# A four-layer graph kernel: layer 0's rows from unscaled relu rows and composite weights, two row blocks begun together, and a listed order

## The chip, the cores and the metric

The kernel runs on one core of one Trainium2 chip. The core has a matrix engine (TensorE, PE in the profile, with its weight loads as PEld), a vector engine (VectorE, DVE), a scalar engine (ScalarE, ACT), a general engine (GpSimd, POOL) and a queue for transfers (SyncE, SP). Each engine works through its own list of instructions in the order in which the program issued them; semaphores make one engine wait for another. The metric is the device time of one execution in microseconds (us). The kernel before takes 595.72 us (median of three runs, 595.17 to 596.13).

## The reference

There are 4096 nodes with 64 features and a sparse 4096 x 4096 matrix of ones and zeros, `adj`. Four layers follow each other, each of the form `x = x + f(relu(layernorm(x)), adj)`. The change touches layer 0 alone:

```
h  = maximum(layernorm(x), 0)
h  = lorentz_linear(h, W,  b,  scale)       # 4096 x 64
q  = lorentz_linear(h, Wq, bq, scale_q)
k  = lorentz_linear(h, Wk, bk, scale_k)
att = adj * sigmoid((2 + 2 * qm @ k.T) / att_scale + att_bias)   # qm: q, column 0 negated
support = att @ h
x = x + support / sqrt(abs(support[:, 0]**2 - sum(support[:, 1:]**2)))
```

`lorentz_linear` multiplies by a 64 x 64 matrix, adds a bias, makes of column 0 a "time" `t = sigmoid(h0) * exp(scale) + 1.1`, and scales columns 1 to 63 so that the sum of their squares is `t*t - 1`. So a positive factor on all of the 63 columns ahead of that scaling is of no consequence to them; the time needs the unscaled column 0. Layer 1 multiplies a counted and decayed `adj` with `h @ weight`, layer 2 multiplies `adj` with `h`, layer 3 averages over neighbours.

## The kernel before

The 4096 rows lie as 32 tiles of 128 rows (`x_sb`, 128 x 32 x 64). A block `ib` is 512 rows (four tiles), and there are eight; a chunk `g` is two tiles of columns, and there are sixteen. The transposed matrix is read from DRAM as tiles of 128 x 1024 for one (block, chunk); GpSimd's queue loads them as one-byte masks (`load_masks`, L180), which stay on the chip for all four layers. Another copy is read by SP's queue to check that all entries are 0 or 1 (`check`, L361); a general program for other matrices stands behind an `If` and is not entered.

**Rows ahead of layer 0** (`before0`, twice: for row tiles 16 to 31, then 0 to 15). Mean, variance and scaling of the rows on VectorE; a transpose to PSUM and a copy (`ht`); a product with W, to which a bf16 split of the biases (`bias_rows`, on GpSimd) is added by a product with ones; factors (`factors`, `root`); `fb` (L758), the rows of h; a second transpose (`hq`) and the product with Wq and Wk together; factors again; query rows into `q_sb` and key rows `kr` (L805); a third transpose into `kt`. The queries of a block are turned by `queries_turned` (L874) and laid out by `queries_laid` (L884).

**Attention of layer 0.** For each (block, chunk): `scores` (L938, PE), `sigmoids` (L951, ACT), `masked` (L962, DVE, a product with the mask), `gather` (L969, PE, into one accumulator per block). I call one `scores` or one `gather` of a (block, chunk) a unit; layer 0 has 128 of each, 256 units. The first block (7) and two units of scores of block 6 stand in a listing with the rows: each part has a planned duration, its predecessors and the PSUM places that it takes, and `Listing.run` tries 2500 random priorities against those planned durations and emits the best plan. Planned idle time of PE is filled with products nobody reads (`idle`, L1062), at first fifty of them. All other units come from a loop, four at a time, with four gathers behind four scores.

**Jobs.** What follows a block is a generator pushed on `jobs` with a lag; `step()` runs the first job to its next `yield` and goes on to the second only when the first has had as many steps as its lag. After a block of attention it is `rows0(ib)` (lag 10): transposes of the accumulator (L236), halves added, the norm of the support, an inverse root on GpSimd (`rsqrt`, L261 to L268: twelve small instructions), the layer norm for layer 1 with a second such root, and `split` (L250, L253), which writes the block's rows for layer 1 into `s2a`. The loop makes one step per unit of scores. Behind layer 0, `chunks_counted` makes eight steps, and layer 1 one step per pass. `need(1, t)` makes steps at once until the block of row tile t is there.

**Layer 1.** Blocks go in pairs; a pass handles two row tiles, from 31 down to 0, of both blocks: products `cnt` (L1260, L1270), the weights `w` (L1284 on DVE, L1286 on ACT), and, one pass late, products `acc` (L1298) with `s2a`. So block 0, finished last in layer 0, is needed last, in the fifteenth products of the first pair.

Of the kernel before, what the change touches and what calls it, by code (L numbers as in the profile page):

```python
# [11 lines left out]
F32 = mybir.dt.float32  # L12
# [27 lines left out]
UP, STEP = 2.0**23, 2.0**11  # L40

# [9 lines left out]
def kernel(  # L51
# [57 lines left out]
    nc.scalar.activation(tried, exp_s[:, 0:1], AF.Sqrt)  # L109
# [29 lines left out]
    def model(general):  # L139
# [9 lines left out]
        HR = 8  # L149
# [5 lines left out]
        def rows_in(gr):  # L155
# [10 lines left out]
        todo = [  # L166
            (ib, g) for ib in order0 for g in (first_cols if ib == order0[0] else range(NG))
        ]
# [201 lines left out]
        pp = pool("pp0", 2, l0, space=PSUM)  # L370
# [3 lines left out]
        for gr in range(1, len(ROWS)):  # L374
            rows_in(gr)
        if not general:
            more_in()

        brow = pro.tile([P, 3 * D], BF16, name="brow" + sfx)
        ones = pro.tile([P, P], BF16, name="ones" + sfx)
        nc.vector.memset(ones, 1.0)

        def bias_rows():
            v = vec[:, V_B : V_B + 3 * D]
            sel = pro.tile([P, 3], F32, name="sel" + sfx)
            high = pro.tile([P, 3 * D], BF16, name="high" + sfx)
            left, part = (
                pro.tile([P, 3 * D], F32, name=f"brow_{a}{sfx}") for a in ("left", "part")  # L390
            )
            total = pro.tile([P, 3 * D], F32, name="brow_sum" + sfx)
            nc.gpsimd.tensor_tensor(sel, ident[:, 0:3], ident[:, D : D + 3], ALU.add)
            for n in range(3):
                nc.gpsimd.tensor_copy(high, v if n == 0 else left)
                to = total if n == 0 else part
                nc.gpsimd.tensor_scalar(to, high, sel[:, n : n + 1], None, ALU.mult)
                if n:
                    nc.gpsimd.tensor_tensor(total, total, part, ALU.add)
                if n < 2:  # L400
                    nc.gpsimd.tensor_tensor(left, v if n == 0 else left, high, ALU.subtract)
            nc.gpsimd.tensor_copy(brow, total)

        class Listing:
# [5 lines left out]

            HOP, TURN, TRIALS = 0.15, 0.12, 2500

# [13 lines left out]
            def plan(self, names, lead):  # L426

                busy, forms, places = {}, {}, dict.fromkeys(names, 0.0)
                at = [part.at for part in self.parts]
                open_ = [len(part.after) for part in self.parts]  # L430
                able = [part for part in self.parts if not part.after]
                where, order, last = {}, [], 0.0
                while able:
                    best = None
                    for part in able:
                        free_at = busy.get(part.engine, 0.0)
                        if forms.get(part.engine) != part.form:
                            free_at += self.TURN
                        t, place = max(at[part.n], free_at), None
                        if part.takes:  # L440
                            free = [(places[n], n) for n in part.takes if places[n] is not None]
                            if not free:
                                continue
                            since, place = min(free)
                            t = max(t, since + self.HOP)
                        if best is None or t - lead[part.n] < best[0]:
                            best = t - lead[part.n], t, part, place
                    _, t, part, place = best
                    if place is not None:
                        places[place] = None  # L450
                    where[part.n] = place
                    part.idle = t - busy.get(part.engine, 0.0)
                    end = busy[part.engine] = t + part.us
                    forms[part.engine] = part.form
                    last = max(last, end)
                    if part.frees is not None:
                        places[where[part.frees.n]] = end
                    able.remove(part)
                    order.append(part)
                    for q in part.then:  # L460
                        at[q.n] = max(at[q.n], end + self.HOP)
                        open_[q.n] -= 1
                        if not open_[q.n]:
                            able.append(q)
                assert len(order) == len(self.parts)
                return last, order, where

            def run(self, names, fill):

                draw = random.Random(1)  # L470
                lead = [0.0] * len(self.parts)
                best = self.plan(names, lead)
                for _ in range(self.TRIALS):
                    other = list(lead)
                    for _ in range(draw.randint(1, 4)):
                        other[draw.randrange(len(other))] = draw.uniform(-2.0, 2.0)
                    plan = self.plan(names, other)
                    if plan[0] <= best[0]:
                        best, lead = plan, other
                self.plan(names, lead)  # L480
                for part in best[1]:
                    part.place = best[2][part.n]
# [3 lines left out]
        def root(y, a, tag):  # L486
# [7 lines left out]
            for share, to in ((SHARE, z), (0.25, y)):  # L494
                nc.vector.reciprocal(q, z)
                nc.vector.scalar_tensor_tensor(q, q, share, a, ALU.mult, ALU.mult)
                nc.vector.tensor_tensor(to, q, z, ALU.add)

        tables, flats = [], []

        TURN = ("pm", "pa")

        def turn_tile(part, name, shape=(P, CI, P)):
            on, tag = (pm, "pr") if part.place == "pm" else (pa0, "pa")
            return on.tile(list(shape), F32, tag=tag, name=name + sfx)

        def before0(todo, gr, bias):
# [13 lines left out]
            def of(u, n=1):  # L521
                return slice(u * HR * n, (u + 1) * HR * n)

# [3 lines left out]
            def numbers(name, n=1):  # L527
                return small(f"{name}{gr}", "", pro, R * n)


            def begin(_):
                v.st, v.va = numbers("st"), numbers("va")
                v.xc, v.sq = buffer("A", "xc", [P, R, D]), buffer("B", "sq", [P, R, D])

            def mean(u):
                def emit(_):
                    if u == 0:
                        begin(_)
# [3 lines left out]
            def scaled(_):  # L542
                nc.vector.tensor_scalar(v.st, v.st, -1.0 / D, None, ALU.mult)

            def centred(u):
                return lambda _: nc.vector.tensor_tensor(
                    v.xc[:, of(u), :], x_sb[:, rows(u), :], bc(v.st[:, of(u)], HR), ALU.add
                )

            def squared(to, frm, part):  # L550
                return lambda _: nc.scalar.activation(
                    getattr(v, to)[:, part, :], getattr(v, frm)[:, part, :], AF.Square
# [6 lines left out]

            def rooted(_):  # L560
                v.rs = numbers("rs")
# [1056 lines left out]
```

## Time and profile before

| | |
|---|---|
| timed runs, median of 3 | 595.72 us (595.17 to 596.13) |
| the profiled execution, first to last instruction | 593.2 us |
| what lies around the span (median less span) | 2.5 us |
| PE busy | 577.5 us (97%) |
| DVE, ACT, POOL busy | 477.9, 337.7, 242.7 us |
| first fifty `idle` products | 1.58 to 15.00 us |
| first scores | 47.83 us |
| block 7 done, loop begins | 83.31 us |
| first `many` (layer 1's counts) | 297.46 us |
| first layer-1 pass | 312.09 us |
| last products of the first pair | 347.37 us |

A row of the timeline is: start, duration, engine, line, operation, tile written and tiles read, size, count. A duration with a count above one is that of the whole stretch. In brackets stands the idle time before and who ended it. PE is nearly always busy, but its busy time includes the `idle` products, and a matmul's end is modelled; what the stage is worth is read from when the useful units run.

### The profile page before, as it was taken

To read this page: it belongs to the slowest core of one execution; us is meant where nothing else is said; L and a number is where in the kernel's file an instruction comes from. 1 tells how busy PE (TensorE), PEld (TensorE's weight loads), DVE (VectorE), ACT (ScalarE), POOL (GpSimd) and SP (SyncE) were. 2 spreads that over 40 slices of the span, in tenths; PEclk is the share of its full clock that TensorE was granted. 3 is DMA by queue.
4 is the path that set the end of the run, shared out by engine and by line. 5 is a ranking of instruction groups with operands and counts; after the bars stand their busy time and mean duration, and the time that the engine had idled before them with its cause. 6 is when DMAs were issued, how large, how long until landed. Compare 5 with 4: busy or idle time off the path is not lost.

```text
span 593.2 us, 9215 instructions
## 1 busy us (share of the span) xinstructions
PE 577.5 (97%) x3138; PEld 238.6 (40%) x3138; DVE 477.9 (81%) x909; ACT 337.7 (57%) x546; POOL 242.7 (41%) x459
## 2 busy tenths in 40 slices
PE   8999999999999999999999999999998999999995
PEld 3663333333333333333243343343443545544553
DVE  5679666899989899999876878879888669987753
ACT  3678666667676776767427677767666014431221
POOL 7625204657767676744434201001010305562352
PEclk9999999999999999999999999999999999999999
DMA  9995932898999899962191545555555486546921
GB/s 148 131 106 45 102 30 18 82 151 136 168 150 166 144 158 153 149 145 88 42 349 38 173 153 189 167 173 177 166 191 181 151 271 200 161 172 210 312 83 42
DMA packets 43016, 87.04 MB, mean 147 GB/s; under 512 B 5136, under 2 KB 22032, under 8 KB 42960
## 3 DMA queue, kind: packets, MB, share of 16 engines
q1 hardware_dynamic: 23808, 68.40, 35.3%
q0 software_dynamic: 18720, 17.57, 31.8%
q8 instruction: 26, 0.43, 0.3%
q10 hardware_dynamic: 432, 0.40, 0.3%
q14 instruction: 30, 0.25, 0.1%
HBM read 135.63 MB, written 1.05 MB: 230 GB/s over the span
## 4 chain that ended last, share of the span: by engine, by line
PE 77%; DVE 10%; POOL 6%; issue 3%; ACT 3%; DMA 1%; DVEq 0%; POOLq 0%; ACTq 0%
PE acc L1370 19%; PE ps L938 12%; PE acc L969 11%; PE acc L1298 10%; PE cnt L1260 9%; DVE att L962 4%; PE cnt L1270 3%; PE idle L1062 3%; PE many L1193 2%; PE pt L236 2%; POOL mask L180 1%; PE pr L1173 1%; POOL rs_a L265 1%; DVE ck L361 1%; PE pn L1447 1%
## 5 line engine op out<-in xcount | busy, mean ns | idle before, releaser
L361 DVE SCALAR_TENSOR_TENSOR ckw<-ckw 128x1024 f32<-128x1024 f32 x98 | 124.5, 1278 | 5.5 <-DMA ckw<-adjt_dram 5.3
L938 PE MATMUL ps<-qt,kt 64*128 64x512 f32 x512 | 123.2, 610 | 2.9 <-DVE att L962 2.5
L969 PE MATMUL acc<-att,fb 128*64 128x512 f32 x512 | 117.8, 599 | 0.6 <-DVE att L962 0.5
L1286 ACT ACTIVATE w<-cnt 128x512 int16<-128x512 f32 x176 | 93.1, 597 | 42.3 <-PE cnt L1270 41.9
L962 DVE TENSOR_TENSOR att<-ps,mask 128x1024 f32<-128x1024 f32 x82 | 98.4, 1217 | 8.4 <-ACT ps L951 8.3
L951 ACT ACTIVATE ps<-ps,att_c,att_a 128x1024 f32<-128x1024 f32 x82 | 93.5, 1177 | 1.5 <-PE ps L938 1.3
L951 ACT ACTIVATE att<-ps,att_c,att_a 128x1024 f32<-128x1024 f32 x46 | 54.6, 1203 | 59.0 <-PE ps L938 58.8
L180 POOL DMA_DIRECT2D mask<-adjt_dram x128 | 70.1, 558 | 19.7 <-DMA mask<-adjt_dram 18.2
L938 PEld LDWEIGHTS ps<-qt,kt 64*128 64x128 f32 x512 | 45.1, 186 | 77.9 <-issue 32.9
L1284 DVE TENSOR_SCALAR w<-cnt 128x512 int16<-128x512 f32 x80 | 53.6, 687 | 23.2 <-PE cnt L1270 21.8
L962 DVE TENSOR_TENSOR att<-att,mask 128x1024 f32<-128x1024 f32 x46 | 56.6, 1246 | 18.1 <-ACT att L951 18.1
L1260 PE MATMUL cnt<-mask,after 128*128 128x512 fp8e4 x256 | 66.3, 379 | 1.9 <-DVE w L1284 1.4
L1298 PE MATMUL acc<-w,s2a 128*128 128x512 bf16 x256 | 66.5, 382 | 0.1
L280 POOL TENSOR_TENSOR xc<-x_sb,st 128x256 f32<-128x256 f32 x24 | 20.0, 832 | 110.1 <-DVE st L277 70.8
L969 PEld LDWEIGHTS acc<-att,fb 128*64 128x64 f32 x512 | 33.5, 136 | 73.0 <-issue 67.5
L1370 PE MATMUL acc<-mask,s2a 128*128 128x512 fp8e4 x256 | 57.8, 379 | 0.0
L1370 PE MATMUL acc<-mask,s2b 128*128 128x512 fp8e4 x256 | 57.7, 379 | 0.0
L265 POOL TENSOR_TENSOR rs_a<-rs_y 128x4 f32<-128x4 f32 x48 | 18.2, 378 | 69.2 <-DVE rs_y L261 66.7
L361 DVE SCALAR_TENSOR_TENSOR ck<-ck 128x512 f32<-128x512 f32 x60 | 43.1, 718 | 0.0
L1260 PEld LDWEIGHTS <-after 128*128 128x128 bf16 x256 | 24.8, 99 | 30.8 <-issue 3.4
L1370 PEld LDWEIGHTS <-s2b 128*128 128x128 f16 x256 | 25.0, 98 | 27.6 <-issue 0.8
L1370 PEld LDWEIGHTS <-s2a 128*128 128x128 f16 x256 | 24.6, 98 | 27.3
(198 smaller groups left out, 606.3 us busy)
## 6 DMA issues: line engine op xcount, KB each, us to landing
ckw<-adjt_dram SPq DMA_DIRECT2D x98, 512.0 KB, 3.5
mask<-adjt_dram POOLq DMA_DIRECT2D x128, 128.0 KB, 9.0
ck<-adjt_dram SPq DMA_DIRECT2D x60, 256.0 KB, 5.9
x_sb<-x_dram SPq DMA_DIRECT2D x4, 256.0 KB, 7.7
out_dram<-y POOLq DMA_DIRECT2D x6, 128.0 KB, 2.2
out_dram<-y ACTq DMA_DIRECT2D x2, 128.0 KB, 2.2
w_sb<-wts_dram SPq DMA_DIRECT2D x2, 80.0 KB, 7.6
vec<-vecs_dram ACTq DMA_DIRECT2D x1, 130.5 KB, 6.3
```

Source lines behind the costliest of these rows:

```text
L180: nc.gpsimd.dma_start(out=masks[ib][:, g * CG : (g + 1) * CG, :], in_=adjt[ib, g])
L265: nc.gpsimd.tensor_tensor(a, y, y, ALU.mult)
L361: nc.vector.scalar_tensor_tensor(at, at, 0.0, at, ALU.not_equal, ALU.not_equal, accum_out=odd[:, k : k + 1])
L938: nc.tensor.matmul(ps[:, c, :], kt[half, g, :], qts[ib][half, :], start=True, stop=True)
L951: nc.scalar.activation(to, ps, AF.Sigmoid, bias=att_c, scale=att_a)
L962: nc.vector.tensor_tensor(att, frm, mask, ALU.mult)
L969: nc.tensor.matmul(acc[c * D : (c + 1) * D, :], lhs[:, t, :], rhs[:, c, :], start=(at == 0), stop=(at == NG - 1), skip_group_check=True,)
L1260: nc.tensor.matmul(cnt, after, masks[ib][:, t, :], start=True, stop=True, skip_group_check=True)
L1284: nc.vector.tensor_scalar(w, cnt, 0.0, None, ALU.max)
L1286: nc.scalar.activation(w, cnt, AF.Relu)
L1298: nc.tensor.matmul(accs[ib], both(s2a, t), w, start=(t == NT - 1), stop=False, skip_group_check=True,)
L1370: nc.tensor.matmul(acc, both(s2, t), masks[ib][:, t, :], start=(t == 0), stop=(t == NT - 1), skip_group_check=True,)
```

## The change

Four things change together.

1. **Rows.** The layer norm's scale is no longer applied. The centred rows are turned at once, relu is taken on the way out of PSUM (`positive`), and the result `r` is multiplied both with W and with composite weights `both_w` = W (column 0 left out) times [Wq, Wk], made by `weights_made` on the chip. What the missing factors would have given is added by small products: the numbers `al` (standard deviation, time, and a common factor) are turned (`numbers_turned`), and multiplied with `spread`, which GpSimd builds from the biases and rows of Wq and Wk. The second transpose (`hq`) goes; two transposes of numbers come. `bias_rows` goes.
2. **The square root** of the variance is no longer ACT's Sqrt but `root` on DVE, so ACT loads one table less in this stage.
3. **Two blocks together.** The listing now holds the sixteen (block, chunk) of blocks 7 and 6 on the first eight chunks, then block 7 on the other eight, and two more scores: 26 units of scores and 24 of gather. Block 6's accumulator holds the PSUM place `pm` meanwhile, so `rows0` of block 7 is held back (`waiting`) until block 6 is done; then both are pushed, with a lag of 16 instead of 10.
4. **The order** of the listing is not planned but read from a list of part numbers, `ORDER`.

The queue of SP gets four small broadcasts (`extra`) ahead of the four loads of `wxn_sb`.

```
+ORDER = (268, 8, 270, 1, 0, 269, 267, 266, 271, 273, 274, 9, 2, 10, 13, 3, 11, 20, 4, 5, 21, ...)
...
-    nc.scalar.activation(tried, exp_s[:, 0:1], AF.Sqrt)
+    nc.scalar.activation(tried, exp_s[:, 0:1], AF.Sigmoid)
...
-        todo = [
-            (ib, g) for ib in order0 for g in (first_cols if ib == order0[0] else range(NG))
-        ]
+        LEAD, FIRST = 2, 24
+        half_cols = [first_cols[: NG // 2], first_cols[NG // 2 :]]
+        todo = [(ib, g) for cols in half_cols for ib in order0[:LEAD] for g in cols]
+        todo += [(ib, g) for ib in order0[LEAD:] for g in range(NG)]
...
+            for j, row in ((1, wts[0:1, W_QK : W_QK + 2 * D]), (2, vecs[:, V_BQK : V_BQK + 2 * D])):
+                nc.sync.dma_start(
+                    out=extra[s + j * CR : s + (j + 1) * CR, :], in_=row.to_broadcast([CR, 2 * D])
+                )
...
+            tail = todo.add("DVE", 0.1, tail, at=1.5)
+            picked = todo.add("POOL", 0.6, picks, at=1.6)
+            for_u = todo.add("POOL", 2.4, spread_out(slice(0, D), vec[:, V_B : V_B + D]), picked, at=7.2)
+            turn = todo.add("PE", 0.5, turn_w, at=8.0, takes=TURN)
+            laid = todo.add("DVE", 0.3, lay_w, turn, tail, frees=turn)
+            product = todo.add("PE", 0.6, multiply_w, laid, takes=TURN)
+            done = todo.add("ACT", 0.9, lay_ww, product, frees=product)
+            for_v = todo.add("POOL", 4.6, spread_out(slice(D, 3 * D), extra), done, picked)
...
+                if lead:
+                    xc.append(add("DVE", 0.7, centred(u), ms[u]))
+                else:
+                    m = add("POOL", 0.2, scaled(u), ms[u])
+                    xc.append(add("POOL", 1.6, centred(u), m))
+            sq = [add("ACT", 0.62, squared(u), xc[u]) for u in HALF]
+            va = [add("DVE", 0.68, variance(u), sq[u]) for u in HALF]
+            va = add("DVE", 0.18, varied, *va)
+            sds = add("DVE", 1.55, rooted, va)
...
+                t = add("PE", 0.5, turned_half(lambda u: v.xc[:, of(u), :], u, "h"), xc[u], takes=TURN)
+                r.append(add("ACT", 0.6, positive(u), t, frees=t))
...
+            hb = add("PE", 1.0, h_added, sT, hs[1], const.for_u)
...
+            sq = [add("ACT", 0.6, h_squares(s), hb) for s in range(2)]
+            zf = add("DVE", 0.2, h_first, *sq, rs)
+            sg = add("ACT", 0.22, h_sigmoid, zf)
...
+            tm = add("DVE", 0.8, h_times, sg)
+            gg = add("DVE", 1.75, h_ratio, tm, *nm)
+            al = add("DVE", 0.2, h_numbers, gg, st)
...
+                pv.append(
+                    add("PE", 1.15, products(u), r[u], const.both, *pv[-1:], takes=WIDE)
+                )
+                vb.append(add("PE", 0.6, added(u), pv[u], aT, const.for_v))
...
             acc, late = first_rows_and_block()
-            push(rows0(order0[0], evacuated(order0[0], acc, 0)), 10)
+            waiting = [(order0[0], evacuated(order0[0], accs[order0[0]], 0))]
...
-            first = [2] * 7 if general else [4, 4, 3, 3]
+            first = [2] * 3 if general else [3, 3]
...
                     if at == NG - 1:
-                        push(rows0(ib, evacuated(ib, acc, 0)), 10)
+                        waiting.append((ib, evacuated(ib, accs[ib], 0)))
+                        for done in waiting:
+                            push(rows0(*done), 16)
+                        waiting = []
```

## The prediction

> **What bounds the kernel now.** I read the busy time by stretches first. Its columns are the stretch, its length, then PE, PEld, DVE, ACT and POOL with their counts, the granted clock, the DMA share and GB/s.
>
> ```profile
> 60.00:80.00 20.00, 19.94 (x86) 6.30 (x88) 12.80 (x11) 12.54 (x14) 4.22 (x8) 1.00 1.02 94
> ...
> 312.00:442.00 130.00, 129.54 (x741) 51.53 (x738) 106.87 (x205) 92.08 (x178) 17.78 (x40) 1.00 0.48 157
> ```
>
> PE bounds both layer 0's attention and layer 1 (129.54 of 130 us), so every microsecond for which PE waits there is lost. The exception is the start, where PE runs fillers while a chain through all engines makes the first keys. So I read the timeline next.
>
> ```profile
> 1.58 13.42 PE L1062 MATMUL idle<-ones 128*128 128x512 bf16 x50 [1.58 <-DVE ones L383]
> ...
> 6.64 7.87 PEld L1062 LDWEIGHTS <-ones 128*128 128x128 bf16 x37 [0.24 <-issue]
> ...
> 14.84 1.04 PE L592 MATMUL pt_h<-ident,xc 128*128 128x128 f32 x8
> ...
> 25.96 0.17 DVE L491 TENSOR_SCALAR nzh<-t2h 128x16 int32<-128x16 int32 x1
> ...
> 27.37 0.17 DVE L497 TENSOR_TENSOR rrh<-nqh,nzh 128x16 f32<-128x16 f32 x1
> ...
> 47.83 1.99 PE L938 MATMUL ps<-qt,kt 64*128 64x512 f32 x8 [0.17 <-ACT kt L607]
> ...
> 51.27 1.89 POOL L805 TENSOR_TENSOR s2a<-tq,rrq 128x512 f32<-128x512 f32 x1 [12.00 <-DVE rrq L497]
> ...
> 54.23 1.07 POOL L805 TENSOR_TENSOR s2a<-tq,rrq 128x512 f32<-128x512 f32 x1
> ```
>
> Three things are to be seen. The fifty fillers end at 15.00, and nothing of PE's comes ahead of them. One `root` of 16 columns takes 27.54 - 25.96 = 1.58 us. The first scores start at 47.83. Last comes layer 1's first pair, where block 0's rows are needed.
>
> ```profile
> 299.52 0.66 PE L236 MATMUL pt<-ident,asb 128*128 128x128 f32 x4
> ...
> 312.05 0.20 POOL L265 TENSOR_TENSOR rs_a<-rs_y 128x4 f32<-128x4 f32 x1 [1.85 <-DVE rs_y L261]
> ...
> 315.41 0.61 POOL L918 TENSOR_TENSOR sup<-sup,rs_y 128x256 f32<-128x256 f32 x1
> ...
> 340.61 0.42 DVE L253 SCALAR_TENSOR_TENSOR s2a<-s2a,xc 128x256 f16<-128x256 f16 x1
> ...
> 343.93 1.03 PE L1260 MATMUL cnt<-mask,after 128*128 128x512 fp8e4 x4
> ...
> 345.21 1.04 PE L1298 MATMUL acc<-w,s2a 128*128 128x512 bf16 x4
> 345.37 3.25 ACT L1286 ACTIVATE w<-cnt 128x512 int16<-128x512 f32 x6 [0.58 <-PE cnt L1270]
> ```
>
> Counting the products from 314.77, the one at 345.21 is the fifteenth, the first that reads block 0. Its rows were ready at 341.0, so before the change there are 4.2 us to spare.
>
> **The start, leg by leg.** I take the order from the changed kernel's queues as built and the durations from rows of before; a hop between engines is 0.15 to 0.2 us.
> - To 15.0: the fifty fillers again stand ahead of PE's first real work, now the turn of W (`pt_w`). The list plans it at 8. DVE's `lay_w` stands ahead of the second `centred`, so that too waits for PE.
> - To 19.9 (4.9): turn 0.35, lay 0.2, centred 0.65, square 0.6, variance 0.65, scale 0.2, root 1.6, four hops.
> - To 22.0 (2.1): numbers turned 0.15 and copied 0.25, two fillers, `h_added` 0.9 (four records, as one unit of scores: 3.63/4).
> - To 27.3 (5.3): two squares 1.15, first column 0.2, sigmoid 0.22, second sum 0.65, times 0.9, ratio 0.4, root 1.6, hops.
> - To 30.8 (3.5): a variance of the other rows (0.65) stands in DVE's queue, then numbers 0.2, turn and copy 0.4, `added` twice 1.8, hops.
> - To 37.5 (6.7): four ACT pieces in turn to 32.7, columns and last sum to 33.9, times 0.6, clip, reciprocal and products 1.2, root of 24 columns 1.75.
> - To 42.0 (4.5): `z1` 0.2, query rows 0.65, time 0.2, transposes 0.4, `queries_laid` 1.5 (as at 45.67), a key time 0.2, `kt` 0.6, hops.
>
> So the first scores start at 42.0, 5.8 us earlier. Not shown before: `spread` for q and k, 2048 elements a lane on GpSimd. By the two product rows (512 elements in 1.07 and 1.89) it takes 4.3 to 7.6; I use 4.5, since DVE waits often there. At 7.6 the other rows' centring, which PE's and DVE's queues stand behind, comes 3 us later and the start is near 45. With no such wait it is 41.
>
> **The two blocks, to 26 units of scores and 24 of gather.** Before has them at 98.8: scores 22 to 25 end at 93.0, the fourth next gather at 96.98, and two more gathers take 1.8. PE's work after: 26 x 0.907 + 24 x 0.895 = 45.1, and 6.5 for the other rows (products 2.1, `added` 1.8, transposes 2.2, fillers 0.4); 51.6 in all. DVE's for the same stretch is 24 x 1.23 + 10 = 40, ACT's 26 x 1.2 + 12 = 43, so both are hidden if their order allows. Not wholly: ACT has 18 us of work in the first ten sigmoids, and block rows 0 to 15's keys come out near 69 where PE is ready at 67.5. I add 2.0, as before shows 2.4 of waits in its own 51.0; bounds 0 and 6. So 95.6: a gain of 3.2 (6.2 at best, a loss of 3.8 at worst).
>
> **The rest of layer 0** keeps its rate (30.95 us a block). Free: the Sqrt table (1.28 us at 21.01 less; ACT's load now lies under the fillers), `bias_rows` (8 us of GpSimd), SP's four broadcasts (0.6 us an issue, landing by 15 where 18 is wanted; the `wxn_sb` loads behind them are used at 295), the masks (24 wanted by 85, loaded 1.27 us apart by 62). If these covers fail, it shows as a later start, which the bound of 45 holds.
>
> **The jobs: a new wait in layer 1.** Two blocks are pushed at once, each with a lag of 16, and the loop makes 16 steps a block. So the list of jobs never catches up: block 1's job begins with the last unit of scores, and block 0's 16 steps later. The eight steps of the counts and seven passes go by first. In the built PE queue block 0's transposes stand behind the seventh products of layer 1, where before they stand in the counts (the row at 299.52). `need(1, 3)` then finds the job unfinished and issues the rest at once, and PE's fifteenth products wait for it. With the times of before: the pass starts at 343.93; DVE has a check and `st`, GpSimd centres by 346.4; ACT's three weights end at 346.95 (half of the row x6), square to 347.4; sum and two small ones to 348.35; the twelve root instructions 3.36 (312.05 to 315.41), as DVE is quiet; scaling 0.43 to 352.2. Ahead of the last piece DVE now has both `degrees_of` (0.16 + 0.25 + 0.23 each, with four PE products between): to 353.65; last piece and hop to 354.3. Wait: 354.3 - 345.21 = 9.1. Bounds 8.0 (no degrees) and 10.1 (root 4.3, as from 324.13). PE has nothing else to do, and its idle time to 515 is 0.46 us (the stretch above) and 1.54 (the next), so hardly anything can be given back.
>
> **The clock after the wait.** The first 13 fillers, on a PE that had been idle, took 5.06 us (1.58 to 6.64); the other 37 took 8.36 to 15.00, or 0.226 each. So 13 x 0.226 = 2.9 would have done, and 2.1 us were lost, though the granted clock reads 1.00 there. No row shows a pause in mid-run, so the bounds are 0 and 2.1; I take 2.1, since this start is the one row of a PE after idleness. The Trainium skill ("TensorE: Matmul & The Clock Gate", Part 1: The HAM clock gate) says that PE falls to half its clock after an idle window of about 3.4 us and needs a busy one to return, which speaks against this change; by it the term would be an estimated 1.7 and the time 603.3.
>
> **Sum**, against the profiled execution: 593.2 - 3.2 + 9.1 + 2.1 = 601.2; with 2.5 around it (595.72 less 593.2) 603.7. Its end of layer 0 comes earlier, layer 1's first pair ends later.
>
> **Rivals.**
> - *The start gains nothing* (0.21): the listing's order, held up by fillers and by GpSimd, gives the first scores at 45 and 4 us more of waits. 98.8 - (45 + 51.6 + 5) = -2.8: 593.2 + 2.8 + 11.2 + 2.5 = 609.7. For it: four engines follow one fixed order. Against: before's rows are used throughout.
> - *PE does not wait for block 0* (0.10), the other side: the chain is fast enough, or its steps come sooner than I count. Then only the start counts: 592.5. It decides when the wait is under 3.2, with no pause long enough to slow the clock. Against: GpSimd's twelve instructions alone take 3.36 and stand behind the pass's own weights.
> - *The clock stays* (within the first case): 601.6, from 593.2 - 3.2 + 9.1 + 2.5.
>
> **How the numbers follow.** My forecast 0.65, the first rival 0.21, the second 0.10, and 0.04 for a sum that comes out even. Time 603.7. The lower end takes a start of 6 and a wait of 9 without the clock (598.7); the upper one is near the first rival (609.5). A measurement of this kernel can tell about 0.2%, 1.2 us, from no change. Slower 0.86, same 0.04, faster 0.10.
>
> **What would show it.** First scores at 41 to 45; 26 and 24 units at about 95.6; in layer 1 one wait of PE at the fifteenth `acc`, ended by DVE's `s2a`, of 8 to 10 us, and after it some products 0.43 apart. Wrong if that wait is short, if products after it keep 0.22, or if the first scores come before 39 or after 46.

## The result, and the profile after

The changed kernel takes 617.37 us (median of 6 runs, 616.08 to 621.71), the kernel before 595.30 us (6 runs, 594.62 to 596.13): 1.0385 times as long, interval 1.0353 to 1.0416. The forecast had the direction and about a third of the size: 8 us more were expected, 22 came.

The profiled execution spans 617.8 us where the sum gave 601.2. It took 620.09 us itself, 2.7 above the median, which is why the "2.5 around it" of the forecast turns into -0.4 here. Landmarks of PE in both traces show where the 16.6 us of span lie:

| | before | forecast | after | missed by |
|---|---|---|---|---|
| first scores start | 47.83 | 42.0 | 46.13 | 4.1 |
| 26 units of scores and 24 of gather done | 98.8 | 95.6 | 99.2 | -0.5 from the row above |
| from there to the end of layer 0 (`pw`, L1211, now L1441) | 198.3 | 198.3 | 204.7 | 6.4 |
| from there to the end of layer 1's first pair | 51.3 | 62.5 | 67.1 | 4.6 |
| from there to the end | 244.8 | 244.8 | 246.8 | 2.0 |

The list of PE's waits in the changed kernel names the places. Its columns are the waiting engine and line, the releaser, the time in total, how often, and the longest.

```profile
PE ps L1157 <- DVE att L1181: 7.3, 6, 1.5
PE pd L1465 <- DVE rdegs L1472: 6.6, 1, 6.6
PE cnt L1490 <- DVE w L1514: 5.2, 3, 2.4
PE pt_sT L726 <- DVE al L508: 3.8, 2, 3.3
PE acc L1528 <- DVE s2a L273: 1.7, 1, 1.7
```

The same list of the kernel before has only the first and the third of these, and shorter:

```profile
PE ps L938 <- DVE att L962: 2.5, 4, 0.6
...
PE cnt L1260 <- DVE w L1284: 1.4, 1, 1.4
```

**The start.** The timeline of the changed kernel around the first root:

```profile
17.37 3.60 POOL L430 TENSOR_TENSOR spread<-pick,extra 128x2048 f32<-128x2048 f32 x1 [5.46 <-ACT extra L562]
17.48 3.72 DVE L656 TENSOR_SCALAR va<-va 128x16 f32<-128x16 f32 x1
...
23.06 0.41 PE L726 MATMUL pt_sT<-ident,al 128*80 128x128 f32 x1 [3.31 <-DVE al L508]
...
24.25 2.07 PE L743 MATMUL ps_h<-spread,sT 16*128 16x512 f32 x4
```

Up to 17.4 the leg keeps to the forecast. Then DVE's scaling of 16 columns, 0.2 in the forecast, takes 3.72: it begins 0.11 after GpSimd's big product and ends 0.23 behind it. The root that follows needs its 1.6, and PE stands still for 3.31. The four products of `h_added`, 0.9 in the forecast, then take 2.07, so PE's clock had gone down: the granted clock is 0.50 from 24 to 28 us.

**The loop.** One of six places of layer 0 where PE waits, on four engines:

```profile
183.24 1.68 POOL L200 DMA_DIRECT2D mask<-adjt_dram  x3
...
184.90 0.77 POOL L264 TENSOR_TENSOR sup<-asb 128x256 f32<-128x256 f32 x1
...
185.70 0.42 ACT L1129 ACTIVATE sq<-sup 128x256 f32<-128x256 f32 x1 [3.21 <-POOL sup L264]
186.03 1.16 ACT L1170 ACTIVATE ps<-ps,att_c,att_a 128x1024 f32<-128x1024 f32 x1
...
187.22 1.23 DVE L1181 TENSOR_TENSOR att<-ps,mask 128x1024 f32<-128x1024 f32 x1 [0.98 <-ACT ps L1170]
...
188.50 1.99 PE L1157 MATMUL ps<-qt,kt 64*128 64x512 f32 x8 [1.53 <-DVE att L1181]
```

GpSimd is busy with the second root of block 6 and three mask loads, so block 5's halves are added late. ACT reaches block 5's square, waits for it 3.21 us, and the sigmoid of the attention (186.03) is queued behind the square. DVE's mask product waits for the sigmoid, and PE for the mask product. Before, PE waited four times, never over 0.63.

**Layer 1, first pass.** A wait that the forecast did not have:

```profile
321.10 0.42 DVE L296 TENSOR_REDUCE st<-x_sb 128x4 f32<-128x256 f32 x1 [3.81 <-POOL x_sb L1138]
...
321.69 0.68 DVE L1514 TENSOR_SCALAR w<-cnt 128x512 int16<-128x512 f32 x1
...
322.42 0.59 PE L1490 MATMUL cnt<-mask,after 128*128 128x512 fp8e4 x2 [2.35 <-DVE w L1514]
...
323.36 1.89 PE L1528 MATMUL acc<-w,s2a 128*128 128x512 bf16 x4
```

Block 1's job now runs beside the first pass. DVE stands 3.81 us at its mean (`st`), because GpSimd has twelve root instructions to do first, and DVE's share of the pass's weights is queued behind. PE waits 2.35, and the next four products take 1.89 where 1.04 is the rule.

**Layer 1, block 0.** The wait that the forecast did have:

```profile
336.59 0.60 PE L256 MATMUL pt<-ident,asb 128*128 128x128 f32 x4
...
363.04 0.25 PE L1465 MATMUL pd<-part,many 128*128 128x4 bf16 x4 [6.58 <-DVE rdegs L1472]
...
365.01 1.89 PE L1528 MATMUL acc<-w,s2a 128*128 128x512 bf16 x4 [1.73 <-DVE s2a L273]
366.69 1.91 PE L1490 MATMUL cnt<-mask,after 128*128 128x512 fp8e4 x4
```

Block 0's transposes stand behind the counts of the seventh pass, as the built queue showed. At the fifteenth products, PE waits 6.58 and 1.73, most of it booked on the degrees that stand in the same DVE queue. Then the products run at half speed (1.89 for 1.04, 1.91 for 1.03), 2.8 us too long in all; the granted clock is 0.51 from 365 to 371.

### The profile page after: what moved, and what is told of

It reads as the page before. It is cut to its first block, busy times and chain, and to the rows that moved or that the text cites. A ratio compares the mean times of both kernels' runs of the same rounds, so it can differ in the third digit from the quotient of the medians.

```text
span 617.8 us, 9211 instructions
## 1 busy us (share of the span) xinstructions
PE 583.7 (94%) x3108; PEld 238.5 (39%) x3108; DVE 488.3 (79%) x945; ACT 334.6 (54%) x545; POOL 248.9 (40%) x465
## 4 chain that ended last, share of the span: by engine, by line
PE 68%; DVE 11%; POOL 9%; issue 4%; ACT 4%; DMA 3%; ACTq 0%; POOLq 0%; DVEq 0%
PE acc L1600 18%; PE acc L1528 9%; PE acc L1188 9%; PE ps L1157 9%; PE cnt L1490 9%; DVE att L1181 4%; PE cnt L1500 3%; PE idle L1289 3%; DMA mask<-adjt_dram 2%; PE many L1423 2%; POOL mask L200 2%; PE pt L256 2%; POOL rs_a L285 2%; POOL rs_a L286 1%; DVE ck L381 1%
## 5 line engine op out<-in xcount | busy, mean ns | idle before, releaser
L1157 PE MATMUL ps<-qt,kt 64*128 64x512 f32 x512 | 125.2, 612 | 7.5 <-DVE att L1181 7.3
L1181 DVE TENSOR_TENSOR att<-ps,mask 128x1024 f32<-128x1024 f32 x76 | 91.1, 1218 | 6.5 <-ACT ps L1170 6.5
L1170 ACT ACTIVATE ps<-ps,att_c,att_a 128x1024 f32<-128x1024 f32 x76 | 86.7, 1175 | 5.1 <-PE ps L1157 5.0
L1170 ACT ACTIVATE att<-ps,att_c,att_a 128x1024 f32<-128x1024 f32 x52 | 61.8, 1202 | 49.1 <-PE ps L1157 47.2
L1181 DVE TENSOR_TENSOR att<-att,mask 128x1024 f32<-128x1024 f32 x52 | 65.4, 1272 | 14.7 <-ACT att L1170 14.6
L1490 PE MATMUL cnt<-mask,after 128*128 128x512 fp8e4 x256 | 68.7, 389 | 5.6 <-DVE w L1514 5.2
L1528 PE MATMUL acc<-w,s2a 128*128 128x512 bf16 x256 | 69.9, 397 | 1.8 <-DVE s2a L273 1.7
L300 POOL TENSOR_TENSOR xc<-x_sb,st 128x256 f32<-128x256 f32 x24 | 19.9, 829 | 102.9 <-DVE st L297 64.4
L381 DVE SCALAR_TENSOR_TENSOR ck<-ck 128x512 f32<-128x512 f32 x60 | 46.4, 773 | 0.0
```

What stands on the lines that cost most here:

```text
L381: nc.vector.scalar_tensor_tensor(at, at, 0.0, at, ALU.not_equal, ALU.not_equal, accum_out=odd[:, k : k + 1])
L1157: nc.tensor.matmul(ps[:, c, :], kt[half, g, :], qts[ib][half, :], start=True, stop=True)
L1170: nc.scalar.activation(to, ps, AF.Sigmoid, bias=att_c, scale=att_a)
L1181: nc.vector.tensor_tensor(att, frm, mask, ALU.mult)
L1490: nc.tensor.matmul(cnt, after, masks[ib][:, t, :], start=True, stop=True, skip_group_check=True)
L1528: nc.tensor.matmul(accs[ib], both(s2a, t), w, start=(t == NT - 1), stop=False, skip_group_check=True,)
```

## The experiments

In the short diffs a `-` line is the changed kernel's (in experiments 2 and 10 that of the kernel before). Line numbers shift by a few from kernel to kernel. A ratio is to the kernel before, which was timed along with each group and took 595.20 to 595.78.

### 1. Jobs pushed with a lag of 10

```
-            rs = rsqrt(inn, tag)
+            rs = rsqrt(inn, tag, key="i")
...
-                            push(rows0(*done), 16)
+                            push(rows0(*done), 10)
```

The own buffers (`key`) are needed because two jobs, this close, would share small ones.

> The changed kernel, with a lag of 10 again instead of 16, and a pair of small buffers of its own for the inverse root of the support, so that two jobs can overlap. Theory A (the held and slowly spaced jobs cost all three late losses: 6.4 us in the loop of layer 0, 15.8 us from the counts to the end of layer 1's first pair, 2.0 us behind it): PE's waits for `rdegs` and `s2a` at the fifteenth products (8.3 us) and for `w` in the first pass (2.35 us) are gone, block 0's transposes stand in the counts again, and the time is 617.4 - 24.2 = 593.2 us, at most 2 us more where two jobs now run together. Rival B (the loop's 6.4 us come from something else, such as the order of the masks or of the checks): the waits in layer 1 go, the six waits of PE for `att` (7.3 us) stay, and the time is 617.4 - 17.8 = 599.6 us. My prediction's own accounting (only the wait of 9.1 us and the clock of 2.1 us belong to the jobs) gives 606.2 us.

Measured: 610.95 us, ratio 1.0243 (1.0216 to 1.0270). Layer 1 behaves as theory A wanted: block 0's transposes are back in the counts (313.41), and nothing of PE's waits at the fifteenth products. But the end of layer 0 comes at 310.99, 7.1 later than after the change (0.7 of it came at the start, the rest in the loop), and that took back half. PE waits for `att` ten times, 11.3 us in all. Two rows of its timeline:

```profile
165.10 0.42 ACT L303 ACTIVATE sq<-xc 128x256 f32<-128x256 f32 x1 [4.11 <-POOL xc L300]
...
171.08 3.52 PE L1157 MATMUL ps<-qt,kt 64*128 64x512 f32 x8 [2.05 <-DVE att L1181]
```

Two jobs closer together make ACT stand longer in a job's square (4.11), and PE's clock goes down as well (3.52 for 1.99). Neither theory had this: the price of a job's place is paid in the loop as well as in layer 1.

### 2. The kernel before, with block 7's job held back

```
-            push(rows0(order0[0], evacuated(order0[0], acc, 0)), 10)
+            waiting = [(order0[0], evacuated(order0[0], acc, 0))]
...
-                        push(rows0(ib, evacuated(ib, acc, 0)), 10)
+                        waiting.append((ib, evacuated(ib, acc, 0)))
+                        for held in waiting:
+                            push(rows0(*held), 16)
+                        waiting = []
```

> The kernel before, with this alone: block 7's job is held until block 6 is done, and all jobs have a lag of 16. Theory A (the jobs alone make the late losses): the loop loses 6.4 us, counts to first pair 15.8 us, the rest 2.0 us, so 595.3 + 24.2 = 619.5 us, with PE waiting for `rdegs` and `s2a` at layer 1's fifteenth products and products of half speed behind it. Rival B (the loop's loss is not of the jobs): 613.1 us. My prediction's accounting: 595.3 + 11.2 = 606.5 us.

Measured: 616.48 us, ratio 1.0365 (1.0339 to 1.0391). Nothing but the two pushes differs from the kernel before, and nearly all of the loss is there, 21 of 22 us. The waits of PE:

```profile
PE ps L938 <- DVE att L962: 6.9, 5, 1.9
PE pd L1238 <- DVE rdegs L1245: 6.6, 1, 6.6
PE cnt L1263 <- DVE w L1287: 3.8, 3, 1.8
PE acc L1301 <- DVE s2a L253: 1.7, 1, 1.7
```

They are the changed kernel's, one by one. Its `pw` comes at 303.34 (6.2 later than before), the end of the first pair 66.2 later (51.3 before), and the rest is as before (245.0). So the late losses need neither the new rows nor the two blocks together: holding the first job back, with a lag of 16, makes them in the kernel before too.

### 3. The second `spread` behind the root

```
-            for_v = todo.add("POOL", 4.6, spread_out(slice(D, 3 * D), extra), done, picked)
+            for_v = todo.add("POOL", 4.6, spread_out(slice(D, 3 * D), extra, pick_v), done, picked)
...
+                if lead:
+                    nc.vector.tensor_scalar(pick_v, pick, 1.0, None, ALU.mult)
```

`pick_v` is a copy that DVE makes right behind the first root, so that GpSimd's product cannot start sooner; `ORDER` has part 7 behind part 18.

> The changed kernel, with the second `spread` (GpSimd, 2048 elements a lane) made to wait until the leading rows' `root` is done: it reads a copy of `pick` that VectorE writes right behind that root. Theory C (VectorE's scaling of `va`, 3.72 us instead of 0.2, stood still because GpSimd was inside its instruction from 17.37 to 20.97): the scaling takes under 0.3 us, the root is done 3.5 us sooner, PE's wait of 3.31 us ahead of `pt_sT` shrinks to under 0.6 and the slow products behind it (`h_added` 2.07, `products` 3.62 us) take 1.1 and 2.1. `spread` now covers the time of the next small sums, which may give 1 us back. First scores at 41 to 44 instead of 46.1, time 613 to 615 us. Rival D (VectorE's instruction was slow for another reason): it is slow wherever it stands, first scores stay near 46, 617 us.

Measured: 616.07 us, ratio 1.0339 (1.0317 to 1.0361). The timeline:

```profile
18.16 0.17 DVE L657 TENSOR_SCALAR va<-va 128x16 f32<-128x16 f32 x1
...
20.27 3.61 POOL L431 TENSOR_TENSOR spread<-pick_v,extra 128x2048 f32<-128x2048 f32 x1 [7.92 <-DVE pick_v L663]
...
21.11 1.13 PE L746 MATMUL ps_h<-spread,sT 16*128 16x512 f32 x4
```

The same scaling now takes 0.17, the numbers are turned at 20.36, without a wait, `h_added` takes 1.13, and the first scores start at 42.71, where the forecast had 42.0. Layer 0 ends 3.3 earlier. Only 1.3 of this reaches the median, so the time lies above C's 613 to 615 though its signs came; in the profiled execution a check's transfer near the end of layer 1 holds PE 3.08 (2.37 after the change).

### 4. Twenty-four fillers for fifty

```
-                for _ in range(int((part.idle - 0.1) / 0.215) if v.filling else 50):
+                for _ in range(int((part.idle - 0.1) / 0.215) if v.filling else 24):
```

> The changed kernel with 24 instead of 50 `idle` products at the start. Theory E (the fillers hold PE's first useful work, `pt_w` at 14.49, and by it VectorE's second centring at 15.29 and all that follows): `pt_w` comes at 9 to 11, the whole chain some 3.5 us sooner, first scores at 42 to 43, time about 613.9 us. Rival F (weights and rows land only near 14 us, or the chain is held by GpSimd's `spread` at a fixed time): first scores stay within 1 us of 46.1, time within 1 us of 617.4; a slower PE behind fewer fillers could even cost up to 2 us.

Measured: 611.46 us, ratio 1.0273 (1.0256 to 1.0290), 2.4 below E's value; F is out. W's turn starts at 10.61 and the first scores at 39.00, 7.1 earlier; layer 0 ends at 296.75 for 303.89. So the fillers did stand ahead of the chain. GpSimd's big product begins here only when DVE's root is over (15.89, idle for 3.91 before), so the two did not meet; the 7.1 us hold this gain as well as the fillers'.

### 5. Jobs pushed with a lag of 17

```
-                            push(rows0(*done), 16)
+                            push(rows0(*done), 17)
```

> The changed kernel with a lag of 17 instead of 16. A job with lag n lets the next one begin n - 1 steps after it, so 16 lets the jobs drift towards each other (transposes 16, 12, 16, 16, 16, 12 steps apart), and 17 keeps them 16 steps apart as before the change. Theory G (the loop's 6.4 us are lost where two jobs come too close: ScalarE stands in a job's square, waiting for GpSimd, and the sigmoids stand behind it): PE's waits for `att` fall from 7.3 us to about 2.5, the loop takes 198 to 200 us from the 26/24 point to the first counts instead of 204.7; block 0's job comes 7 steps later, so the wait in layer 1 grows from 8.3 to 14 to 18 us. Time 617.4 - 5.5 + 8 = about 620 us (615 to 625). Rival H (the loop's loss comes of the jobs being late, wherever they stand): waits for `att` stay at 7 us, and the time is 625 us or more.

Measured: 616.79 us, ratio 1.0358 (1.0341 to 1.0376). With a lag of n the next job starts n - 1 steps later, and its transposes wait for the edge of four units. So at 16 the blocks' transposes stand 16, 12, 16, 16, 16, 12 and 15 steps apart in the emitted order; the trace has block 6's at 150.46 and block 5's at 173.29, 22.8 us where a block takes 31. At 17 the first five distances are 16. The loop gets 3.3 shorter (201.4), and PE's waits for `att` fall from 7.3 to 4.3. Block 0 is later for it: 10.29 and 1.65 at the fifteenth products. The total is G's, its terms are not: G had 198 to 200 for the loop, 2.5 for the waits and 14 to 18 for layer 1.

### 6. The lag by the block

```
-                            push(rows0(*done), 16)
+                            push(rows0(*done), 16 if general else {2: 10, 1: 6, 0: 10}.get(done[0], 17))
```

With it go own root buffers, another pool for block 0's centred rows, and two steps in `split` for all blocks.

> The changed kernel with jobs 16 steps apart in the loop (lag 17), and the last three close together where layer 0 has ended: lags 10, 6 and 10 for blocks 2, 1 and 0, small buffers of their own for the support's inverse root, another buffer for block 0's centred rows, and two free steps less ahead of the last piece of blocks 1 and 0. Theory A with G (held jobs cost all of the late losses, by their closeness in the loop and by their lateness in layer 1): no wait at layer 1's fifteenth products, waits for `att` near 2.5 us, the time 593 to 597 us, which is the kernel before within 0.5%. Rival B (something else of the change slows the loop): 599 to 602 us.

Measured: 610.53 us, ratio 1.0257 (1.0242 to 1.0273), above both forecasts. The loop keeps 200.9 and the fifteenth products wait for nothing, but the first pass waits 4.60, now for ACT:

```profile
320.60 0.42 ACT L1129 ACTIVATE sq<-sup 128x256 f32<-128x256 f32 x1 [9.11 <-POOL sup L264]
...
322.04 0.58 PE L1490 MATMUL cnt<-mask,after 128*128 128x512 fp8e4 x1 [4.60 <-ACT w L1516]
```

ACT stands 9.11 us at block 0's square with three of the pass's weights behind it. The pattern is the loop's, in another place. Near the end of layer 1 a check's transfer holds PE 3.50 here.

### 7. PE kept awake in block 0's wait

```
+                    for n in (30, 8):
+                        for _ in range(n if first else 0):
+                            nc.tensor.matmul(rest, after, masks[7][:, 0, :], start=True, ...)
+                        need(1, t)
```

Thirty-eight products that nobody reads are added ahead of the fifteenth ones; nothing is left out.

> The changed kernel, with 38 products that nobody reads put into PE's queue around the wait for block 0 in layer 1, 30 ahead of the degrees and 8 ahead of the fifteenth products. They take the place of idle time. Theory K (the half speed behind the wait, 1.89 instead of 1.04 us for four products, comes of PE's idleness): the fifteenth products and the counts behind them take 1.04 and 1.03 us at once, 2.8 us are saved, 0.4 of it spent on later degrees: 615.0 us. Rival L (the slow products have another cause, such as the reading of rows just written): they stay at 1.9, and the time stays at 617.4.

Measured: 614.60 us, ratio 1.0322 (1.0307 to 1.0337). The timeline:

```profile
356.86 6.65 PE L1533 MATMUL rest<-mask,after 128*128 128x512 fp8e4 x30
...
365.90 0.81 PE L1538 MATMUL acc<-w,s2a 128*128 128x512 bf16 x3
```

Products behind the stretch run at full speed, and 2.8 us are saved, the excess counted above. So that part of the loss is the clock's, and not a slower supply of weights.

### 8. to 10. All mended, and the kernel before with fewer fillers

Experiment 8 joins 3, 4 and 6. Experiment 9 takes 36 fillers and a lag of 8 for block 1. Experiment 10 is the kernel before with 36 fillers.

```
+                for _ in range(int((part.idle - 0.1) / 0.215) if v.filling else 36):
...
+                            push(rows0(*done), 16 if general else {2: 10, 1: 8, 0: 10}.get(done[0], 17))
```

> The changed kernel with three things mended: the jobs as in the run of the same call (lag 17, the last three close), 24 fillers instead of 50, and the second `spread` behind the first root. By theory: the start gains 7 us on the changed kernel (first scores at 39.0, as with 24 fillers), so the 26/24 point is at 92 instead of 98.8 before; the loop and layer 1 are those of the kernel before. Time 595.7 - 6.7 = 589 us, and up to 593 if a few waits stay. If the loop is slowed by something else of the change: 595.

Measured: 600.97 us, ratio 1.0086 (1.0054 to 1.0117), above all values expected. PE runs out of fillers 2.42 us before W has landed, and its products take twice as long from 10.75 to 27.7 (granted clock 0.52); the first scores slip to 43.2. The first pass waits 4.74, as in 6.

> The changed kernel mended once more: 36 fillers (the 24 left PE idle for 2.4 us ahead of `pt_w`, after which it ran at half speed up to 27.7), the second `spread` behind the first root, jobs 16 steps apart in the loop, and at the end of layer 0 lags of 10, 8 and 10 for blocks 2, 1 and 0, so that block 0's square stands behind the weights of layer 1's first pass in ScalarE's queue and not ahead of them. Theory: first scores at 39 to 40, no wait of 4.7 us in layer 1's first pass and no half speed behind it, block 0's rows ready about 4 us ahead of the fifteenth products. Against the run with 24 fillers (601.0): 3.5 us at the start, 5 to 8 us in layer 1, so 590 to 593 us, faster than the kernel before (595.2). Rival: ScalarE or VectorE stands in another step of the three close jobs and the wait only moves: 597 to 601 us.

Measured: 596.88 us, ratio 1.0025 (1.0014 to 1.0036), next to the rival's 597 to 601. First scores 38.83; 26 and 24 units are done at 92.0, 6.8 earlier than before. The loop takes 201.0, 2.7 of that back, and layer 0 ends at 292.96, 4.1 earlier than before. Then the first pass waits 2.63 for DVE's `w`, as after the change, and the 4 us are gone.

> The kernel before with 36 fillers instead of 50, as a control: how much of what fewer fillers bring belongs to the changed rows. Before, the rows ahead of PE's first transposes are ready at 13.2 and 13.8 and the transposes start at 14.84, so at most 1.6 us can be had: 593.6 to 595.2 us by theory E. If the gain is as large as in the changed kernel (5.9 us with 24 fillers), fewer fillers are worth it by themselves and the change has no part in it: 589 us.

Measured: 596.24 us, ratio 1.0017 (1.0007 to 1.0028); first scores at 47.29. Fewer fillers alone bring the kernel before nothing: its first transposes come 1.4 us earlier (13.39 for 14.84), its first scores 0.5.

### 11. The new rows with one block first

The listing's own planner and one block first, as before; 36 fillers, the second `spread` later, lag 10.

```
-        LEAD, FIRST = 2, 24
+        LEAD, FIRST = 1, NG
...
+            push(rows0(order0[0], evacuated(order0[0], accs[order0[0]], 0)), 10)
```

> The changed rows (composite weights, numbers turned, `spread` behind the first root, 36 fillers) without the two blocks and without the written order: block 7 first, then two scores of block 6, as before the change, ordered by the planner of the kernel before, jobs pushed as before with a lag of 10. Theory A: with the jobs as before, the loop takes 30.95 us a block and layer 1's first pair 36.3 us, with no wait at its fifteenth products; the rest depends on the planned order, which puts the second `spread` behind the rows of h: first scores between 40 and 46, and the wait for the keys of rows 0 to 15 some 2 to 4 us longer than with two blocks. Time 592 to 597 us. If the late losses came of the rows themselves (new order of VectorE's and GpSimd's work), it would be above 605 us.

Measured: 607.77 us, ratio 1.0207 (1.0193 to 1.0222). The planner puts the second `spread` at 30.17, and the first scores start only at 55.24; `pw` is 12.5 later than before. From `pw` on everything is as before: 51.6 to the end of the first pair, and in the loop four waits of 0.62 or 0.63. The time lies where the expectation put the other case (above 605), but by these landmarks the loss is all ahead of `pw`: the late losses do not come with the rows. How fast the rows are with one block first and a good order stays open.

### 12. Block 1's mean one step later

```
+            if ib == 1 and not general:
+                yield
             h = yield from norm(rows, None, tag, False)
-            yield from split(h, s2a, rows, 2)
+            yield from split(h, s2a, rows, 1 if ib == 0 and not general else 2)
```

This is experiment 9 with `w` ahead of `st` on DVE, and a lag of 9 for block 1.

> The start and the loop mended as before (36 fillers, the second `spread` later, jobs at distances 10, 9 and 10), and now block 1's mean (`st`) one step later, so that DVE's weights of layer 1's first pass stand ahead of it, with block 0's steps one later again. The whole is computed. If the wait of 2.63 us and the slow products behind it are what kept the earlier kernel level with the one before, they go: no wait over 1 us before the end of the first pair, all products at 1.03 or 1.04 for four, that end near 345, a span of 589 to 590.5 and a time of 591.5 to 593.5. Rival: the wait only moves, as ACT's square of block 0 or block 0's last piece is late next, and the time stays at 596 to 597.

Measured: 596.77 us, ratio 1.0025 (1.0016 to 1.0034): the rival again. The timeline:

```profile
312.70 0.94 DVE L273 SCALAR_TENSOR_TENSOR s2a<-s2a,xc 128x256 f16<-128x256 f16 x1 [3.64 <-POOL s2a L270]
...
314.89 0.59 PE L1495 MATMUL cnt<-mask,after 128*128 128x512 fp8e4 x2 [3.02 <-DVE w L1519]
```

The wait moved from the first pass to the second. DVE now stands 3.64 at block 2's last piece, for the same GpSimd, with the next weights behind. GpSimd has to do the roots and additions of three blocks there, and in 6, 9 and 12 whichever instruction of DVE or ACT reads it first holds up the pass. No version tried beats the kernel before.

## Why the forecast was right and wrong

**Right.**
- *The wait at block 0.* Place, releaser and size: 8.3 us and 0.25 of products between, where 9.1 was the sum and 8.0 to 10.1 the bounds. GpSimd's twelve root instructions took 3.30 (359.17 to 362.47), 3.36 in the sum. That the lag makes it is shown by 1 (shorter: gone) and 5 (longer: 11.9).
- *The two blocks.* From the first scores to 26 and 24 units it took 53.1; 51.6 and 2.0 were forecast.
- *The order of the legs at the start.* With one instruction moved (3) the first scores come at 42.71.

**Wrong.**
- *"The rest of layer 0 keeps its rate."* It lost 6.4 us, the largest miss. The step counted the jobs' lag where block 0 is late, and not in the loop, where the same lag moves jobs to 12 steps apart and to other places within the block. Experiment 2 shows it with nothing else changed (6.2). How much of it the holding back and how much the longer lag makes was not separated; with the first job held and a lag of 10 (experiment 1) the loop is slower still. Experiment 5 gives 3.3 of it back by the distance alone. The other 3 us of the loop are only partly placed: 1.8 of it are waits for `att` over those of before, 1.3 are open.
- *"To 19.9 ... scale 0.2", and `spread` "since DVE waits often there".* The price of `spread` was below both bounds (3.60, not 4.3 to 7.6). The step that failed is the 0.2: DVE was not waiting at that moment, and its scaling stood 3.5 us for GpSimd. With the slow clock behind it (`h_added` 2.07 for 0.9) this is most of the 4.1 of the table: 3 gives 3.4 of it back, 0.7 stay. The Trainium skill ("SBUF — State Buffer", Who interferes with whom) says that DVE's `tensor_scalar` can take the ports that it shares with GpSimd, and that the one that issues second then waits for the whole of the other's instruction. The two rows at 17.37 and 17.48 agree, with 0.17 for the same instruction in 3.
- *"The jobs: a new wait in layer 1", one where there were two.* Block 1's job was counted to begin at the end of layer 0, but what it does to the first pass was not. DVE's `st` ahead of `w` cost 2.35, the slow products behind it 1.6. Experiments 9, 6 and 12 show the same wait for DVE's `w`, for ACT's `w` and one pass later. From `pw` to the end of the first pair 15.8 us were lost where 11.2 were forecast; these two with the wait at block 0 and the slow products behind it make 15.0, and 0.8 is not placed.
- *"The clock after the wait", 2.1.* The mechanism was right, its size too small: 2.8, measured by the rows and by 7. The upper bound came from the start, where the slow stretch was 5.06 us; in layer 1 it goes on for 6, from 365 to 371. The forecast read no pause in mid-run in the kernel before; there are two short ones, 1.72 ahead of `pw` at 297.10 and 1.40 at 453.41, with the clock at 1.00 behind both. The clock also went down after the first pass's wait, which the forecast had not asked about.
- *Behind the first pair*, nothing was forecast and 2.0 came: DVE waits 1.34 for a check's transfer (0.38 before), PE 2.37 for DVE (1.40 before), and the products behind run slow. This wait is from 1.35 to 3.50 in the kernels here; what moves the transfer was not tried.

The first rival (609.7) named the right fault of the start, an order "held up by fillers and by GpSimd", but no rival had the loop. (Its sum adds 5 us to the 51.6 where its words have 4 more than the 2.0 of the forecast, which is 6; with that it would be 610.7.) The bound of 45 us for the first scores was passed as well (46.13), by the wait and the clock together, where only the wait had been bounded.

## What to carry to other kernels

When work is deferred by a queue of generators, its lag decides which engines meet: write out the emitted steps for every block, not only for the last, and look in each engine's queue for what is in front of the instruction on the critical path. An engine that runs in order and reads a slow engine's result holds back everything behind it; such a wait, once moved, is found again at the next reader, so look for the slow producer. And price a pause of PE with the slow products that follow it.

## What the runs showed of the hardware

- Pauses of PE of about 2 us can slow what follows, and their length alone does not decide. Behind 1.83 (experiment 2) and 2.35 four products of layer 1 took 1.89 for 1.04, behind 2.05 (experiment 1) eight of `scores` took 3.52 for 1.99. But behind 2.08, three microseconds earlier, four kept 1.13, and behind 2.07 (experiment 3) and 2.83 (experiment 5) the next products kept full speed too. A pause of the changed kernel in its timeline:

```profile
476.92 1.01 PE L1490 MATMUL cnt<-mask,after 128*128 128x512 fp8e4 x2 [2.37 <-DVE w L1514]
...
478.41 1.88 PE L1528 MATMUL acc<-w,s2a 128*128 128x512 bf16 x4
```

Behind 2.37 two products take 1.01 for 0.59 and the next four 1.88; the row at 188.50, shown for the loop, keeps 1.99 behind 1.53.

- The clock of the traces shows what decides. It is 1.00 or 0.50, and in each trace its changes lie whole multiples of 3.41 us apart: in the changed kernel it is 0.50 from 22.76 to 29.59, 323.13 to 326.55, 360.68 to 370.92 and 476.73 to 480.15. So the spans can be divided into pieces of 3.41 us along these changes. Where PE was idle for 1.90 us or more of a piece at 1.00, the next piece was at 0.50, in all 26 cases of the fourteen traces between the first and the last change; with less idle time the clock stayed, with two exceptions (1.75 in experiment 2, 1.34 at the start of experiment 4). The 2.35 of the first pass lies in one piece; the 2.07 of experiment 3 lies across two (0.90 and 1.17), and the 2.83 of experiment 5 too (1.75 and 1.08). Three pieces of the changed kernel, with the columns of the prediction's first view:

```profile
319.72:323.13 3.41, 1.06 (x8) 0.27 (x6) 1.23 (x3) 0.93 (x2) 2.56 (x4) 1.00 0.30 100
323.13:326.55 3.42, 3.42 (x12) 1.03 (x8) 1.29 (x2) 1.39 (x3) 0.00 (x0) 0.50 0.00 0
326.55:329.96 3.41, 3.41 (x21) 1.28 (x21) 1.95 (x5) 2.15 (x5) 0.92 (x5) 1.00 0.00 0
```

The Trainium skill ("TensorE: Matmul & The Clock Gate", Part 1: The HAM clock gate) speaks of an idle window of about 3.4 us. The length of the pieces agrees, but pieces idle for little more than half were enough, so here the measurement decides.

- So a slow stretch lasts one or more such pieces: one after 2.35 (1.6 us lost), three around the wait of 8.3 (2.8 us lost behind it), and five, 17 us, after a pause of 2.42 at the start of experiment 8, where the work behind it came in smaller parts. Why those five did not end sooner is not shown.
- A DVE instruction of 16 columns can take 3.72 us beside a GpSimd product of 2048 elements a lane, and 0.17 alone. At 33.95 and 34.84 of the changed kernel two more small ones take 0.85 and 0.97, for 0.17 and 0.18, beside GpSimd's two `fb` products (33.73 to 35.78). Not every DVE instruction stands: in experiment 3 two reductions at 20.25 take 1.22 together beside the same product, as they do at 23.12 in the changed kernel without it.
